# Which engine issues the DMAs that send off ScalarE's results, in a four-layer selective-scan kernel

## The chip, the cores and the metric

The kernel runs on one core of one Trainium2 chip. The metric is the device time of one execution in microseconds (us), the median of several runs. The core's engines have their own instruction streams, in order: TensorE (PE; its weight loads are the row PEld), VectorE (DVE), ScalarE (ACT), GpSimd (POOL) and SyncE (SP), which computes nothing and here issues every DMA.

## What is computed

The input is x, 2 images of 96 channels x 96 x 96. Four layers follow each other; each adds to x what it makes of x's group norm:

```python
x = x + _L0_conv_ref(_gn(x), ...)   # windows of 6 x 6, sampled at learned offsets
x = x + _L1_conv_ref(_gn(x), ...)   # gated sum of four directions
x = x + _L2_conv_ref(_gn(x), ...)   # rows and columns in snake order
x = x + _L3_conv_ref(_gn(x), ...)   # rows and columns, plain order
```

Every layer projects to 192 channels, makes delta, B and C from them, and runs a selective scan in four directions over the 9216 pixels of each image (layer 0: over its windows), with 16 states for each channel:

```python
dA = exp(delta * A); h = h * dA + (delta * u) * B; y = sum over states of h * C
```

The four directions are summed (with D * u), normed or gated, multiplied by silu(z), and projected back to 96 channels. All is float32.

## The kernel before, in words

**Jobs and steps.** A job is one direction over one chunk of T positions (T = 288 in layer 0, class Windows, 256 jobs; T = 384 in layers 1 to 3, Gated, Snake and Plain, 192 jobs each). `Machine.scan` (L385) runs the jobs of a machine, one after the other, in steps; a job has 8 of them (4 groups of 4 states, two halves of 96 channels). Layer 0 has a machine of its own; the other three share a second one and follow each other without a break.

One step n holds, for 128 partitions (32 channels x 4 states, three such blocks side by side): the products dB = w * B on DVE (tile `pd`), the scan on DVE (`hs`), three exponentials on ACT that make `dA` of the next step, and, from the second machine on, two small ACT copies that carry the state from chunk to chunk: `hc`, the scan's last column, and `w`, that column put at the ends of the next w tile. POOL multiplies the scan by C (`hC`), and PE sums over the states (`py`) and spreads B over the partitions (`pb`).

**The preamble** (L321) makes what a job's scan needs, some 10 to 19 steps ahead, a piece a step. PE projects the job's input (`pm`), ACT copies the result to the tile `p` (its rows 64 to 79 are C), and C is stored to a scratch tensor in HBM. PE and ACT then make `v`, delta, with a softplus at its end; it is stored to HBM too. POOL multiplies v by the input, and the product `du` is stored as well. These three are read back by the loads C<-C, d<-delta and w<-du, which spread one row over several partitions: in each job 4 loads of C and, in `spread` (L396), 6 of d and 6 of w, three for each half. In Gated C is multiplied by the gate on POOL before it is stored (L334).

**Sums and directions.** `Cross.jobs_of` (L949) holds what the trunk's jobs do at their end. For direction 0 and 2 ACT copies the sum from PSUM to `y`, and `store` (L990) sends it to HBM (`yc`, `yr`). For direction 1 DVE adds the sum stored before, PE turns the result, ACT copies it to `turn`, and it goes to `yt`. Direction 3 reads those back and ends in the layer's output.

**Stages.** Before a layer's scans can begin, its input is prepared in chunks: normed, projected, filtered, passed through silu. `stage_conv` (L1076) does that for Snake and Plain and stores `flat` and `sz`; every sixth chunk `leave` (L937) stores the columns gathered in the tile `big` to `flatc`, a piece a step. `Gated.stage` (L1191) stores `xn`, the gates `gc` and `gr`, `sz` and, through `leave`, `xc`. The first of these stages runs alone, before the second machine's scans begin (`at_once`, L1397); the rest runs in the background of the scans.

**The order of the work.** The order on each engine is that in which the program is written: the class `Engine` (L146) ties each instruction to the one before it on its engine. Generators are advanced once a step, in `scan`, in a fixed order: first the loads, sums, exponentials and copies of the step, then the ACT work that `act` (L260) put off from the step before (`slot`), then DVE's products and scan, then the preambles, then the background (`hop`, L531). All instructions go through the helper at L156, so the profile shows L156 for nearly every one, and groups are told apart by their tiles.

**What holds SP.** SP takes its DMAs in the program's order. A store waits until its tile is made, and every DMA behind it waits with it. Buffers are few: one `v`, two `p`, three or four `d` and `w`, three C tiles, three slots of each scratch tensor in HBM.

Of the kernel before, what the change touches and what calls it, by code (L numbers as in the profile page):

```python
# [145 lines left out]
class Engine:  # L146


    def __init__(self, tc, engine):
        self.tc, self.engine, self.last = tc, engine, None  # L150
# [61 lines left out]
class Machine:  # L212
# [6 lines left out]

    def __init__(self, ctx, tc, nc, const, T, dram):
        self.tc, self.nc, self.const, self.T, self.dram = tc, nc, const, T, dram
        self.E = E = 0 if T == 288 else 1
        pool = lambda name, bufs, **k: ctx.enter_context(tc.tile_pool(name=f"T{T}{name}", bufs=bufs, **k))
        self.w = pool("w", 1)
        self.sb = pool("sb", 2)
        self.pm = pool("pm", 1, space=PSUM)
        self.pb = pool("pb", 1, space=PSUM)
        self.pd = pool("pd", 1, space=PSUM)  # L230
        self.py = pool("py", 2, space=PSUM)
        if not E:
            self.po = pool("po", 1, space=PSUM)
        self.B = [self.pb.tile([128, 512], F32, tag=f"pb{i}", name="pb") for i in range(2)]
        self.bg, self.low = [], []
        self.turn = 0
        self.now, self.taken, self.used, self.slot = None, None, None, []
# [83 lines left out]
    def preamble(self, j, n):  # L321


        nc, k, layer = self.nc, j.k, j.layer
        T, E = self.T, self.E
        yield from j.gather(j)
        xs = j.xs

        j.p = self.p[n % 2]
        self.own()  # L330
        m = self.mm(self.ps(80)[:, :T], [(layer.wx[:, k, h, :], xs[:, h, :]) for h in range(2)])
        self.act(lambda m=m: nc.scalar.copy(j.p[:, E : E + T], m))
        yield
        if j.gate is not None:  # L334
            C = j.p[64:80, E : E + T]
            nc.gpsimd.tensor_mul(C, C, j.gate[64:80])
            yield
        j.C = self.dram.tile([N, T], F32, tag=f"C{T}", name="C", bufs=3)
        nc.sync.dma_start(j.C, j.p[64:80, E : E + T])
        v = self.t2("v", 1)  # L340
        for h in range(2):
            self.own()
            m = self.mm(self.ps()[:, :T], [(layer.dtw[:, k, 96 * h : 96 * h + 96], j.p[:R, E : E + T])])
            c = layer.scol[:, 2 * k + h : 2 * k + h + 1]
            self.act(lambda h=h, m=m, c=c: nc.scalar.activation(v[:, h, :], m, AF.Identity, bias=c))
            if h == 0:
                yield
        self.act(lambda: nc.scalar.activation(v, v, AF.Softplus))
        yield
        scratch = lambda tag: self.dram.tile([2, 96, T], F32, tag=f"{tag}{T}", name=tag, bufs=3)  # L350
        j.delta, j.du = scratch("delta"), scratch("du")
        nc.sync.dma_start(j.delta.rearrange("h p t -> p h t"), v)
        yield
        du = self.t2("du", 1)
        nc.gpsimd.tensor_mul(du, v, xs)
        nc.sync.dma_start(j.du.rearrange("h p t -> p h t"), du)
        if E:
            j.h = self.sb.tile([128, NG, 3], F32, tag="hc", name="hc", bufs=3)
        yield
        if j.gate is not None:  # L360
            nc.gpsimd.tensor_mul(xs, xs, j.gate.unsqueeze(1).to_broadcast([96, 2, T]))
# [539 lines left out]
class Cross(Layer):  # L901
# [35 lines left out]
    def leave(self, im, c, to, hs):  # L937

        if c % self.group < self.group - 1:
            return  # L940
        rows = slice(4 * (c - self.group + 1), 4 * (c + 1))
        for h in range(hs):
            for w in range(0, S, 16):
                at = slice(w, w + 16)
                self.nc.sync.dma_start(to(h, at, rows), im.big[:, h, at, :])
                yield


    def jobs_of(self, im):  # L949
        nc, T, nch = self.nc, self.T, self.nch  # L950
        jobs = []
        for way in range(4):
            order = range(nch)[:: -1 if way % 2 else 1]
            for c in order:
                at = slice(T * c, T * (c + 1))

                def gather(j, way=way, c=c):
                    assert im.staged, (self.n, im.b, self.now, im.__dict__.get("at"))
                    return self.gather(im, j, way, c)

                def late(j, g, way=way, c=c, at=at):
                    if way == 3 and g == 2:
                        j.turned = self.sb.tile([S, 4, 192], F32, tag="turned", name="turned", bufs=1)
                        nc.sync.dma_start(j.turned, im.yt[4 * c : 4 * c + 4].rearrange("r c k -> c r k"))
                    if way % 2 and g == 5:
                        j.old = self.t2("old", 1)
                        o = (im.yc if way == 1 else im.yr)[:, :, at]
                        nc.sync.dma_start(j.old, o.rearrange("h p t -> p h t"))

                def add(j, h, q, yp, way=way):  # L970
                    if q == 0 and (self.n == 1 or way == 2):
                        nc.tensor.matmul(yp, self.diag[:, h, :], j.xs[:, h, :], start=True, stop=False)
                        return True
                    if q > 1 and way == 3:
                        for r in (2 * q - 4, 2 * q - 3):
                            eye = self.const["rev" if self.snake and r % 2 == 0 else "eye"]
                            nc.tensor.matmul(
                                yp[:, S * r : S * r + S], j.turned[:, r, 96 * h : 96 * h + 96], eye,
                                start=False, stop=False,
                            )  # L980
                    return False

                def finish(j, h, yp, way=way, c=c):
                    if h == 0:
                        j.y = self.t2("y", 3)
                    self.finish(j, way, h, yp, j.y)
                    if h:
                        self.m.bg.append(store(j.y, way, c))

                def store(y, way, c):  # L990
                    at = slice(T * c, T * (c + 1))
                    yield
                    if way == 3:
                        yield from self.end(im, c, y)
                        return
                    if way != 1:
                        nc.sync.dma_start((im.yc if way == 0 else im.yr)[:, :, at].rearrange("h p t -> p h t"), y)
                        return
                    turned = self.sb.tile([S, 4, 192], F32, tag="turn", name="turn", bufs=1)
                    for h in range(2):  # L1000
                        yield from self.spare()
                        p = self.px()
                        for i in range(4):
                            nc.tensor.transpose(
                                p[:, S * i : S * i + S], y[:, h, S * i : S * i + S], self.const["eye"]
                            )
                        nc.scalar.copy(
                            turned[:, :, 96 * h : 96 * h + 96], p[:, : 4 * S].rearrange("p (i k) -> p i k", i=4)
                        )
                        yield  # L1010
                    nc.sync.dma_start(im.yt[:, 4 * c : 4 * c + 4, :], turned)

                jobs.append(
                    Job(self, self.ks[way], way % 2 == 1, c == order[0], gather, finish, late if way % 2 else None, add)
                )
        return jobs
# [59 lines left out]
    def stage_conv(self, im):  # L1076
        nc, T, b = self.nc, self.T, im.b
# [25 lines left out]
        def tail(c, tiles):  # L1103
# [4 lines left out]
            yield  # L1108
            yield
            for t, to in zip(tiles, (im.flat, im.sz)):  # L1110
                nc.sync.dma_start(to[:, :, T * c : T * (c + 1)].rearrange("h p t -> p h t"), t)
            while im.left < c:
                yield
            big = self.columns(im, c)
# [57 lines left out]
class Gated(Cross):  # L1172
# [18 lines left out]
    def stage(self, im):  # L1191
# [12 lines left out]
        def chunk(c):  # L1204
# [17 lines left out]
            self.act(lambda: affine(big, xn.rearrange("p (r c) -> p c r", c=S)))  # L1222
            yield
            yield
            nc.sync.dma_start(im.xn[:, T * c + 3 : T * c + T + 3], o)

            z = self.t2("cz")
            for h in range(2):
# [40 lines left out]
            self.act(lambda: nc.scalar.activation(g.rearrange("p k r -> p r k"), e, AF.Exp))  # L1269
            yield  # L1270
            yield
            nc.sync.dma_start(im.gc[:, :, 4 * c : 4 * c + 4].rearrange("k c r -> c k r"), g)
            p, act = yield from self.either(16)
            nc.tensor.transpose(p[:, :S], g.rearrange("p k r -> p (k r)"), self.const["eye"])
            gt = self.sb.tile([16, S], F32, tag="gt", name="gt")
            act(lambda p=p: nc.scalar.copy(gt, p[:, :S]))
            yield
            yield
            nc.sync.dma_start(im.gr[c], gt)
            yield from self.step(7, 0, 4)  # L1280
            self.act(lambda: nc.scalar.activation(z, z, AF.Silu))
            yield
            yield
            nc.sync.dma_start(im.sz[:, :, at].rearrange("h p t -> p h t"), z)
            yield from self.leave(
                im, c, lambda h, w, r: im.xc[:, 3 : L + 3].rearrange("p (c r) -> p c r", r=S)[:, w, r], 1
            )
# [179 lines left out]
```

## Time and profile before

| what | value |
|---|---|
| median of 3 runs | 29051.85 us (29048.37 to 29093.39) |
| the profiled execution's own time | 29109.88 us |
| its span, and granted TensorE clock | 29108.1 us, 0.646 |
| DVE busy | 25162.6 us (86%) |
| PE busy, PE weight loads | 22199.9 us (76%), 6987.2 us (24%) |
| ACT busy | 18935.5 us (65%), of which 2837 table loads 3639.9 us |
| POOL busy | 18851.4 us (65%) |
| DMA packets' share of the 16 engines' span | 42.7% on one queue, q1 |
| DVE scan, Snake and later | 2.57 us each; product `pd` 1.37 us |

The page gives the busy time of each engine over the whole span, and groups of instructions by tiles as out<-in. Waits are put down to what ended them: "ACT dA <- DMA d<-delta" is idle time of ACT before a dA instruction that the landing of the load of d ended. SPq is SP's queue: an issue that waits. Durations of DMA issues on SP are those of the issue, not of the transfer; the time to landing is given apart.

### The profile page before, as it was taken

The numbers are of one execution on the slowest core, as the hardware profiler recorded it, in microseconds if no ns is written. First come the engines' busy times: TensorE is split into PE (matmuls) and PEld (weight loads), VectorE is DVE, ScalarE is ACT, GpSimd is POOL, SyncE is SP. The second block draws the span as 40 slices with busy tenths as digits, with TensorE's granted clock in tenths as the row PEclk, the third lists the DMA queues.
The fourth block names the chain that finished last, engine by engine and source line by source line (L and its number), as shares of the span: only waits on it lengthen the run. The fifth ranks groups of instructions, "written<-read, shape, count | busy, mean of one in ns | idle before, by whom it ended". The sixth has DMA issues, their size and how long they took to land. (4 is left out here: it accounts for less than half of the span.)

```text
span 29108.1 us, 269563 instructions
## 1 busy us (share of the span) xinstructions
PE 22199.9 (76%) x72312; PEld 6987.2 (24%) x72312; DVE 25162.6 (86%) x15459; ACT 18935.5 (65%) x40441; POOL 18851.4 (65%) x9508
## 2 busy tenths in 40 slices
PE   7887888888567777777777777777777778776778
PEld 2222333333112222222222221212222122221112
DVE  7888888888457788877889999999999989999999
ACT  5666666666567676676666776566765666665566
POOL 5777767777446566765676666666666656666667
PEclk7666666666566676777776675556765577555556
DMA  3333333333344445444444544454444544444444
GB/s 97 101 101 101 101 97 100 98 100 97 69 95 128 125 129 147 149 134 133 136 145 147 147 143 135 142 157 143 145 142 143 155 143 141 146 140 134 134 134 141
DMA packets 3285863, 3707.11 MB, mean 127 GB/s; under 512 B 756928, under 2 KB 3260518, under 8 KB 3284232
## 3 DMA queue, kind: packets, MB, share of 16 engines
q1 hardware_dynamic: 3284328, 3689.86, 42.7%
q8 instruction: 570, 9.34, 0.1%
q14 instruction: 965, 7.91, 0.1%
HBM read 2933.04 MB, written 755.57 MB: 127 GB/s over the span
## 5 line engine op out<-in xcount | busy, mean ns | idle before, releaser
L156 POOL TENSOR_TENSOR hC<-hs,C 128x1152 f32<-128x1152 f32 (+1 forms) x6656 | 15603.3, 2345 | 8616.7 <-PE py L156 4214.1
L156 DVE TENSOR_TENSOR_SCAN hs<-dA,pd 128x1158 f32<-128x1158 f32 (+1 forms) x6656 | 15830.0, 2378 | 1059.8 <-ACT hc L156 115.2
L156 ACT ACTIVATE dA<-d,w_alog 128x384 f32<-128x384 f32 (+1 forms) x19968 | 10306.6, 580 | 6643.8 <-DVE hs L156 5725.8
L156 PE MATMUL py<-hC,zs 128*32 128x384 f32 (+1 forms) x39936 | 7797.5, 677 | 2754.2 <-POOL hC L156 2648.8
L156 DVE TENSOR_TENSOR pd<-w,pb 128x1158 f32<-128x1158 f32 (+1 forms) x6656 | 8465.7, 1272 | 1624.9 <-PE pb L156 548.7
L156 PE MATMUL pb<-p,sel 16*128 16x386 f32 (+1 forms) x6656 | 4151.6, 715 | 485.3 <-ACT cz L156 172.1
L156 ACT ACT_TABLE_LOAD x2837 | 3639.9, 1283 | 108.6 <-DMA w_alog<-in_L_alog 44.4
L156 PE MATMUL pm<-p,w_dtw 6*96 6x384 f32 (+1 forms) x3328 | 2237.7, 768 | 1714.6 <-ACT p L156 982.8
L156 PEld LDWEIGHTS py<-hC,zs 128*32 128x32 f32 x39936 | 1212.2, 129 | 7886.4 <-POOL hC L156 4900.9
L156 PE MATMUL pm<-x,w_in 128*96 128x384 f32 (+1 forms) x2554 | 1514.6, 747 | 996.4 <-ACT p L156 802.9
L156 PEld LDWEIGHTS pb<-p,sel 16*128 16x128 f32 x6656 | 1363.4, 254 | 2681.9 <-issue 1009.7
L156 PE MATMUL pm<-x,w_taps 96*96 96x384 f32 x3456 | 1508.1, 580 | 42.0 <-ACT xs L156 23.8
L156 PE MATMUL po<-xp,w_off 96*96 96x288 f32 x4608 | 1443.3, 460 | 26.8 <-ACT t L156 25.0
L156 PE MATMUL pm<-xs,w_wx 96*80 96x384 f32 x2304 | 1398.6, 753 | 46.3 <-DVE o L156 16.1
L156 PEld LDWEIGHTS pm<-p,w_dtw 6*96 6x96 f32 x3328 | 588.5, 230 | 3328.4 <-ACT p L156 1474.0
L156 ACT COPY w<-hc 128x6 f32<-128x6 f32 x4416 | 830.5, 194 | 499.7 <-DMA w<-du 458.9
L156 ACT ACTIVATE v<-pm,w_scol 96x384 f32<-96x384 f32 (+1 forms) x1664 | 910.3, 547 | 245.9 <-PE pm L156 171.3
L156 POOL TENSOR_TENSOR du<-v,xs 96x768 f32<-96x768 f32 x576 | 1045.0, 1814 | 10.5 <-ACT v L156 10.5
L156 PEld LDWEIGHTS pm<-x,w_in 128*96 128x96 f32 (+1 forms) x2554 | 562.9, 243 | 1973.5 <-ACT p L156 1001.0
L156 PEld LDWEIGHTS po<-xp,w_off 96*96 96x96 f32 x4608 | 791.6, 181 | 658.1 <-issue 342.0
L156 PEld LDWEIGHTS pm<-x,w_taps 96*96 96x96 f32 x3456 | 611.1, 192 | 938.8 <-issue 721.4
L156 ACT COPY hc<-hs 128x3 f32<-128x3 f32 x4608 | 830.7, 180 | 5.7 <-DVE hs L156 5.7
(213 smaller groups left out, 13159.9 us busy)
## 6 DMA issues: line engine op xcount, KB each, us to landing
d<-delta SPq DMA_DIRECT2D x3456, 192.0 KB, 3.3
w<-du SPq DMA_DIRECT2D x3456, 192.0 KB, 3.4
C<-C SPq DMA_DIRECT2D x2304, 192.0 KB, 3.4
d<-delta SPq DMA_DIRECT2D x1536, 144.0 KB, 2.6
w<-du SPq DMA_DIRECT2D x1536, 144.0 KB, 2.6
delta<-v SPq DMA_DIRECT2D x576, 288.0 KB, 2.7
du<-du SPq DMA_DIRECT2D x576, 288.0 KB, 3.4
C<-C SPq DMA_DIRECT2D x1024, 144.0 KB, 2.7
```

Of the source, the lines that this page charges most:

```text
L156: r = traced(*args, **kwargs)
```

## The change

The stores of what ScalarE has made last are issued by ScalarE's own instruction stream instead of SyncE's. These are C where it is not gated, delta, the sums of directions 0 and 2, the turned sums, and the stages' rows, columns, gates and silu(z). Loads stay on SP, and so do the stores of du, of the gated C, of Snake's `ysum` and of the layers' outputs, which other engines make or finish. Nothing else changes; the positions in the program's order are the same.

```diff
@@ preamble
-        nc.sync.dma_start(j.C, j.p[64:80, E : E + T])
+        (nc.scalar if j.gate is None else nc.sync).dma_start(j.C, j.p[64:80, E : E + T])
...
-        nc.sync.dma_start(j.delta.rearrange("h p t -> p h t"), v)
+        nc.scalar.dma_start(j.delta.rearrange("h p t -> p h t"), v)
@@ leave
-                self.nc.sync.dma_start(to(h, at, rows), im.big[:, h, at, :])
+                self.nc.scalar.dma_start(to(h, at, rows), im.big[:, h, at, :])
@@ jobs_of, store
-                        nc.sync.dma_start((im.yc if way == 0 else im.yr)[:, :, at].rearrange("h p t -> p h t"), y)
+                        nc.scalar.dma_start((im.yc if way == 0 else im.yr)[:, :, at].rearrange("h p t -> p h t"), y)
...
-                    nc.sync.dma_start(im.yt[:, 4 * c : 4 * c + 4, :], turned)
+                    nc.scalar.dma_start(im.yt[:, 4 * c : 4 * c + 4, :], turned)
@@ stage_conv, tail
-                nc.sync.dma_start(to[:, :, T * c : T * (c + 1)].rearrange("h p t -> p h t"), t)
+                nc.scalar.dma_start(to[:, :, T * c : T * (c + 1)].rearrange("h p t -> p h t"), t)
@@ Gated.stage
-            nc.sync.dma_start(im.xn[:, T * c + 3 : T * c + T + 3], o)
+            nc.scalar.dma_start(im.xn[:, T * c + 3 : T * c + T + 3], o)
...
-            nc.sync.dma_start(im.gc[:, :, 4 * c : 4 * c + 4].rearrange("k c r -> c k r"), g)
+            nc.scalar.dma_start(im.gc[:, :, 4 * c : 4 * c + 4].rearrange("k c r -> c k r"), g)
...
-            nc.sync.dma_start(im.gr[c], gt)
+            nc.scalar.dma_start(im.gr[c], gt)
...
-            nc.sync.dma_start(im.sz[:, :, at].rearrange("h p t -> p h t"), z)
+            nc.scalar.dma_start(im.sz[:, :, at].rearrange("h p t -> p h t"), z)
```

## The prediction, made before the changed kernel ran

> **What bounds the kernel now.** I read the busy time of each engine stage by stage first, because the page's average (DVE 86%) hides that the stages differ. The boundaries are where the scans of a stage start and end. Columns after the stretch and its length: busy us (instructions) of PE, PEld, DVE, ACT, POOL, then the clock, the DMA share and GB/s.
>
> ```profile
> 0.00:7644.00 7644.00, 6117.86 (x22754) 2269.89 (x22754) 6542.28 (x4915) 4695.90 (x8829) 5362.07 (x3027) 0.65 0.34 99
> 7644.00:8279.00 635.00, 264.89 (x548) 99.93 (x542) 28.22 (x76) 355.90 (x529) 62.10 (x168) 0.50 0.35 38
> 8279.00:15784.00 7505.00, 5728.54 (x18078) 1794.36 (x18079) 6182.19 (x3403) 5163.86 (x10781) 4819.78 (x2431) 0.72 0.46 137
> 15784.00:22436.00 6652.00, 5058.59 (x15670) 1432.18 (x15669) 6190.69 (x3604) 4432.10 (x10601) 4220.60 (x1881) 0.62 0.48 144
> 22436.00:29108.00 6672.00, 5029.98 (x15270) 1390.82 (x15269) 6219.22 (x3464) 4287.75 (x9704) 4386.86 (x2003) 0.60 0.46 141
> ```
>
> The rows are Windows, the staging before Gated's scans ("staging"), Gated, Snake and Plain. VectorE (DVE) sets the pace: 86%, 82%, 93% and 93% in the scan stages. All its idle time is 1102, 600, 1330, 461 and 451 us in that order. ScalarE (ACT) is 61%, 56%, 69%, 67% and 64% busy: second to DVE nowhere but close to the path where its work comes in heaps, in Gated above all.
>
> Next I read who waits for whom: first SP's own waits, then ACT's and DVE's in Gated (us in total, times, longest).
>
> ```profile
> SPq L156 <- ACT w L156: 6342.3, 873, 18.8
> SPq L156 <- ACT v L156: 3095.3, 393, 19.6
> SPq L156 <- DMA du<-du: 2075.6, 832, 4.9
> SPq L156 <- DMA delta<-v: 1454.4, 832, 2.7
> SPq L156 <- ACT p L156: 1270.2, 285, 73.6
> SPq L156 <- ACT y L156: 922.6, 250, 14.0
> ```
>
> SP stands before ACT's results: v, p and y (5288 us) and, in smaller rows of the same view, cz, o, gg and gt (260.6, 213.8, 112.4, 12.9), 5888 us in all. Those waits leave SP with the change. The largest, ACT w, is a load waiting for its buffer and stays.
>
> ```profile
> ACT dA L156 <- DMA d<-delta: 589.7, 192, 9.3
> ...
> ACT w L156 <- DMA w<-du: 256.0, 186, 5.2
> ...
> DVE pd L156 <- ACT w L156: 286.2, 174, 10.5
> ```
>
> These are the two places where a late load shows in Gated: ACT idles 846 us before d and w, and DVE feels some of it through w.
>
> **What leaves SP, and what that gains.** 2528 of SP's 19506 issues move: 832 delta, 640 C (the 192 of Gated stay), 288 y (yc, yr), 144 yt, 96 flat, 144 sz, 192 flatc, 48 each of xc, xn, gc and gr. Summing their own durations in the trace gives 949 us of SP issue. The Trainium skill, DMA: Bandwidth & Descriptors, section "Issuing engines are not separate DMA queues", speaks against more than that: DMAs of all issuers run on the same 16 engines, and a second issuer saves only the sequencer's issue time. The waits row would promise up to 5888 us by standing SP free, the rule only part of 949. So I took every idle time over 0.15 us of ACT, DVE or PE that a landing load ended, and followed SP back from that load while its issues stood end to end. The run's head is almost always a w<-du load that waits for du to land, or a d or w load that waits for its buffer; it is a moved store in single cases only. In the runs stand 185 us of moved issues: 0 in Windows, 15 in staging, 49 in Gated, 67 in Snake, 54 in Plain. That bears out the rule: the loads behind delta wait for delta's landing (1454.4 us over 832) whoever issues it, and delta goes out 0.02 to 0.03 us after the softplus already. What of the 185 reaches DVE: in Gated DVE waits 306 us for w and dA (286.2 and 20.0) against ACT's 846, so 36%; in Snake 38 of 161 us, 23%; in Plain 33 of 299, 11%. 49 x 0.36 + 67 x 0.23 + 54 x 0.11 = 39 us; with staging's 15 whole, a gain of 54 us. Bounds: 0; and 185 whole, plus 43 for DVE's late x strips in Windows (55.8 less its first wait of 12.7), 228 us.
>
> **What each issue costs ACT.** No DMA on ACT is in this trace. The nearest rows are the same step's on SP; here twice the softplus that makes delta.
>
> ```profile
> 10021.22 0.84 ACT L156 ACTIVATE v<-v 96x768 f32<-96x768 f32 x1
> 10021.97 0.18 ACT L156 COPY w<-hc 128x6 f32<-128x6 f32 x1
> 10022.08 0.32 SPq L156 DMA_DIRECT2D delta<-v  x1
> 10022.17 1.28 ACT L156 ACT_TABLE_LOAD   x1
> ...
> 10023.46 1.63 ACT L156 ACTIVATE dA<-d,w_alog 128x384 f32<-128x384 f32 x3
> ...
> 10024.99 0.18 ACT L156 COPY hc<-hs 128x3 f32<-128x3 f32 x1
> 10025.26 2.57 DVE L156 TENSOR_TENSOR_SCAN hs<-dA,pd 128x1158 f32<-128x1158 f32 x1 [0.20 <-ACT hc L156]
> ```
>
> Start us, duration, engine, operation. After the change the delta issue stands between v and the copy into w, and waits for v on ACT itself. Queued behind it are w (DVE's pd waits for it), the table load, the next step's three dA and the hc copy (the scan waits for both). The price of one such "draining" issue: ACT loses the 0.09 us by which v and the copy overlap here, waits 0.02 (v ends at 10022.06, SP starts at 10022.08), issues for 0.31 (median of delta; C 0.318, y 0.311) and starts again 0.04 later (after an ACT semaphore wait that idled it the next instruction starts 0.04 later): 0.46 us. In this step the end of hc sets the scan, so DVE pays all of it. In Snake the same step leaves room: dA ends at 11.21, its scan starts at 13.12.
>
> ```profile
> 20009.58 1.63 ACT L156 ACTIVATE dA<-d,w_alog 128x384 f32<-128x384 f32 x3
> ...
> 20013.12 2.57 DVE L156 TENSOR_TENSOR_SCAN hs<-dA,pd 128x1158 f32<-128x1158 f32 x1
> ```
>
> There 1.91 us of room cover 0.46, and nothing is paid. Over all steps the room between dA's end and its scan is 2.6 to 3.5 us in the median, in Gated under 0.2 us for the tightest tenth.
>
> C, delta and y drain (SP issues them 0.02 us after the producer, in the median). The others (yt, flat, sz, flatc, xc, xn, gc, gr) are written a yield or more after their data: SP issues them 3 to 27 us after (gc 0.9, xn 2.2). For these the skill, Advanced Engine Details and Errata, section "Sequencer Loop", says that engine instructions can be read and queued while microcode executes: the datapath works on, price 0. But the trace shows how short that lead is: an ACT semaphore instruction ends 0.28 us (median) before the next ACT instruction starts, against some 0.40 of issue. I take 0.20, between 0 and a draining issue of 0.55 (0.40 plus the 0.15 above).
>
> How many are paid? ACT gets 2528 issues, 1760 draining, 768 other: 1760 x 0.46 + 768 x 0.20 = 963 us, but most falls into its 5726 us of waiting for the scans. To separate, I followed each of DVE's 1909 idle times over 0.15 us (2747 us together) back through its releasers to the DVE instruction before, and counted the moved issues that lie inside an ACT part of that path, at the time SP issues them now. Draining ones: 36 in Windows (33 delta), 148 in Gated, 33 in Snake, 26 in Plain, 243 in all. Others: 176 in Gated (149 are flat and sz of Snake's staging), 81 in staging, 12 else, 269. So 243 x 0.46 = 112 and 269 x 0.20 = 54: a loss of 166 us. Ends: 243 x 0.31 and nothing for the others, 75; 243 x 0.7 and 269 x 0.55, 318.
>
> One piece is counted by itself: in staging the six xc stores stand together on SP, one burst over 14.87 us (at 7941.34). On ACT they come one a round between compute: 24 at the tile's median 0.59, 14 us; 0 to 59 (four bursts whole).
>
> What remains costs nothing: descriptors, bytes and the loads on SP are the same. du stays on SP behind POOL and the d loads, so POOL's and SP's order to each other changes only by the gaps. If ACT's cover in Snake and Plain were gone, their 1342 issues would cost up to 1342 x 0.46 = 617 us; 1.9 us of room say they don't.
>
> **Sum.** 166 + 14 - 54 = +126 us on the profiled execution's 29109.88 (span 29108.1 and 1.8 around it): 29236. That execution is 58 us above the median of the runs, 29051.85, so I forecast 29052 + 126 = 29178, say 29180.
>
> **Rivals.**
> - *Late loads come forward (faster).* In Gated SP's heaps of d and w issue set the path: 378 loads late there. If the moved issues ahead of them and those behind it pass whole to DVE (228 us), and ACT's price is at its low end, 75, the time is 29052 - 153 = 28900. It decides from the point where the gain of 54 passes the loss, that is if DVE gets over three quarters of it. For it: 5888 us of SP's standing; against: no run's head is a moved store. Chance 0.23, mostly nearer -90 (28960).
> - *All of it falls into ACT's idle time.* Then DVE's waits stay, and the time is within 58 us, 29052. For it: 35% of ACT is idle; against: 324 moved issues on the path in Gated. 0.14.
> - *An issue is dearer on ACT than on SP*, because two issuers meet (SP issues 36% of the span) or it queues full, as flatc (up to 1.69 us) and xc (up to 4.54) do: with 0.3 us more on each of the 512, +154, and the burst whole, +45: about 29380. 0.15.
> - *It doesn't move at all* can't be: every line edited runs.
>
> **Chances.** Some 0.2% (58 us) is what a measurement of this kernel can tell from no change. The likeliest case, +126, has 0.48: its own range is 29070 to 29330, and 0.08 of it falls within 58 us. Slower: 0.40 + 0.15 = 0.55. Same: 0.14 + 0.08 = 0.22. Faster: 0.23. The range takes the loss's high end with the burst (318 + 59 = 377, 29430) and reaches most of the way to the gain's end: 28930.
>
> **What would show it.** Right: ACT's issues appear at 0.31 us with 0.02 before and 0.04 after; SP's rows for v, p and y are gone and C<-C loads go out sooner, with nobody waiting less; the row of d<-delta keeps most of its 590 us in Gated; DVE's waits for ACT (w, hc, dA) grow there, by some 100 us. Snake and Plain change by under 40 us each. Wrong: if d and w waits in Gated fall by half, SP's standing did delay loads, in a way that its runs did not show. If Windows loses more than 50 us, the C and delta issues reach DVE through PE (its pm and pb matmuls wait for ACT's p and v), which I counted only where DVE already waits.

## The result, and the profile after

The changed kernel takes 29023.84 us (median of 16 runs, 29006.44 to 29044.35); the kernel before takes 29112.42 us on the same chip (16 runs, 29048.37 to 29169.14). The ratio is 0.9969, with a 95% interval of 0.9962 to 0.9976: about 90 us, or 0.31%, **faster**. The forecast was 29180 us and slower. The time lies in the predicted range, the direction does not. Run again later, on one chip with new runs of the kernel before, the same kernel gained less: 0.9987 (0.9977 to 0.9997; after2 below). The profiled execution took 29007.22 us (span 29005.0, clock 0.649).

Busy time by stage after the change, in the columns of the prediction's first fence (Windows, staging, Gated, Snake, Plain):

```profile
157.00:7572.00 7415.00, 5924.64 (x22554) 2193.13 (x22552) 6511.07 (x4853) 4661.37 (x8783) 5334.79 (x2987) 0.66 0.34 101
7572.00:8188.00 616.00, 257.70 (x545) 96.77 (x542) 29.37 (x77) 355.46 (x529) 62.24 (x169) 0.51 0.36 40
8188.00:15649.00 7461.00, 5763.07 (x18077) 1809.52 (x18078) 6179.94 (x3403) 5178.17 (x10779) 4819.36 (x2430) 0.72 0.47 137
15650.00:22327.00 6677.00, 5073.84 (x15668) 1437.35 (x15667) 6189.19 (x3603) 4468.06 (x10598) 4219.64 (x1880) 0.62 0.48 143
22328.00:28978.00 6650.00, 5028.66 (x15242) 1388.67 (x15240) 6213.89 (x3456) 4313.83 (x9691) 4377.68 (x1996) 0.60 0.47 141
```

From the first scan of a stage to its last, before and after: Windows 7488.1 to 7414.7 (-73), staging 637.0 to 615.9 (-21), Gated 7501.4 to 7460.6 (-41), Snake 6650.0 to 6676.5 (+26), Plain 6645.0 to 6649.5 (+5). DVE's work is the same in each; what changed is how long it stands. In these two executions the largest piece is in Windows, for which the forecast had only a loss.

The moved issues appear on a queue of their own (page, part 3: packets, MB, share of 16 engines). The two shares add up to 43.1%, against 42.7% on q1 alone before: the traffic is the same.

```profile
q1 hardware_dynamic: 2566248, 3207.82, 36.4%
...
q10 hardware_dynamic: 718080, 482.05, 6.7%
```

SP's own waits (us in total, times, longest):

```profile
SPq L156 <- DMA delta<-v: 8075.2, 832, 82.8
SPq L156 <- POOL hC L156: 5646.1, 1380, 9.7
SPq L156 <- DMA du<-du: 2220.1, 832, 7.0
```

The rows for v, p and y are gone or next to nothing (p 0.8 us), as forecast. But SP does not stand less: all its rows add up to 19048 us, against 17854 before. It now stands before delta's landing (8075.2 us over the same 832 loads, 1454.4 before), most likely because the d load behind delta's store comes up for issue earlier and waits for the same data. The row "ACT w", 6342.3 us before, which I said would stay, shrinks to 10.1 us, while "POOL hC" grows from 400.0 to 5646.1: a row names only the last of several releases.

In Gated, ACT's waits (first fence) and DVE's (second):

```profile
ACT dA L156 <- DMA d<-delta: 518.9, 192, 8.6
...
ACT w L156 <- DMA w<-du: 205.1, 180, 5.7
...
ACT w L156 <- ACT v L156: 55.3, 135, 0.9
...
ACT L156 <- DMA w<-du: 20.0, 6, 4.3
...
ACT w L156 <- DMA d<-delta: 14.7, 5, 5.2
```

```profile
DVE pd L156 <- ACT w L156: 238.0, 177, 7.2
DVE pd L156 <- PE pb L156: 186.2, 142, 3.5
DVE hs L156 <- ACT hc L156: 110.5, 117, 1.7
DVE pd L156 <- ACT hc L156: 83.8, 42, 3.9
```

Loads of d and w do come earlier. The two rows of the prediction's second fence fall from 845.7 to 724.0 us together; part of that only stands in other rows, which are new (the last two of the fence, and 4.4 us at cz). ACT's waits for these loads in all fall from 846 to 763 us, and DVE's wait for w from 286.2 to 238.0. "ACT w <- ACT v" is new too: the price of delta's issue. DVE's waits for hc grow (94.5 to 110.5 and 36.1 to 83.8).

A softplus of delta in Gated, as in the prediction's third fence:

```profile
9966.92 0.84 ACT L156 ACTIVATE v<-v 96x768 f32<-96x768 f32 x1
9967.80 0.31 ACTq L156 DMA_DIRECT2D delta<-v  x1
9968.15 0.20 ACT L156 COPY w<-hc 128x6 f32<-128x6 f32 x1 [0.38 <-ACT v L156]
9968.37 1.28 ACT L156 ACT_TABLE_LOAD   x1
```

The issue starts 0.04 us after v, takes 0.31, and ACT's datapath idles 0.38 us where the two instructions overlapped by 0.09 before.

### The profile page after: what moved, and what is told of

Read it like the earlier page. It is cut to its first block, busy times and chain, and to the rows that moved or that the text cites. A ratio compares the mean times of both kernels' runs of the same rounds, so it can differ in the third digit from the quotient of the medians.

```text
span 29005.0 us, 268196 instructions
## 1 busy us (share of the span) xinstructions
PE 22131.0 (76%) x72312; PEld 6968.5 (24%) x72312; DVE 25159.9 (87%) x15459; ACT 19020.5 (66%) x40441; POOL 18853.2 (65%) x9508
```

## The experiments

Two theories of the gain. **Late loads**: SP, rid of 2528 issues, gets the loads out earlier (the prediction's first rival). **Clock**: in Windows TensorE's granted clock swings, and the change shifts ScalarE against that swing. Each kernel below is the kernel before with the edit named; times are medians, ratios against runs of the kernel before on the same chip. Lengths of stages are of single profiled executions.

### Windows: what the profile shows

Windows does its work in strips of 64 scans. Most of them take close to 232.1 us in both kernels. Before, 11 of 31 took over 236 us; after, 1. Here are the first 25 us of three neighbouring strips before (busy PE, PEld, DVE, ACT, POOL, then the clock, DMA share and GB/s), which go on to take 239.0, 245.3 and 232.8 us:

```profile
3635.50:3660.50 25.00, 25.00 (x72) 11.25 (x70) 14.57 (x12) 9.82 (x18) 9.50 (x6) 0.58 0.20 58
3874.50:3899.50 25.00, 25.00 (x63) 10.98 (x64) 12.91 (x10) 9.81 (x18) 8.29 (x5) 0.50 0.20 58
4119.80:4144.80 25.00, 24.94 (x112) 12.06 (x110) 21.19 (x17) 13.58 (x26) 14.36 (x8) 0.91 0.32 95
```

And the two strips of the changed kernel that lie at the same place, 232.2 and 232.1 us long:

```profile
3643.50:3668.50 25.00, 24.94 (x116) 12.36 (x116) 21.86 (x17) 13.91 (x26) 14.30 (x8) 0.97 0.33 96
3875.60:3900.60 25.00, 24.94 (x116) 12.41 (x115) 22.22 (x17) 13.91 (x26) 14.39 (x8) 0.97 0.28 82
```

A strip begins with a heap of PE work (the offset matmuls `po` of the next strip), on which DVE waits. Where the clock is 0.5 to 0.6 there, PE gets through 63 to 72 matmuls instead of 112 to 116, and DVE does 13 to 15 us of work instead of 21 to 22. The same matmuls, before (first) and after; the bracket is DVE's wait before the instruction:

```profile
3880.25 4.16 PE L156 MATMUL po<-xp,w_off 96*96 96x288 f32 x8
...
3886.83 0.67 DVE L156 TENSOR_TENSOR yn<-y,py 96x288 f32<-96x288 f32 x1 [3.93 <-PE py L156]
```

```profile
3879.67 2.18 PE L156 MATMUL po<-xp,w_off 96*96 96x288 f32 x8
...
3883.20 0.69 DVE L156 TENSOR_TENSOR yn<-y,py 96x288 f32<-96x288 f32 x1 [0.33 <-PE py L156]
```

Eight matmuls of one shape take 4.16 us or 2.18. The record of the clock alternates between 0.5 and 1.0 in multiples of 3.413 us, and its pattern repeats with the strip (correlation with itself 232 us later: 0.75 before, 0.86 after; 232.1 us are 68 of these 3.413). The strips differ in when the clock rises: before, within 4.3 us of the strip's start in the short ones, and 17.4 to 34.5 us after it in all 11 long ones. PE is recorded as busy throughout those 17 to 35 us, so its busy time doesn't tell what delays the rise; that stays open. That a late rise makes a strip long holds in all 20 profiles that have Windows: of 600 strips (the first of each profile left out) 52 had a clock under 0.66 in their first 25 us, and all took over 236 us; the other 548 had 0.90 or more, and 6 of them took over 236.

### Windows: which part of the change does it

**w_only**: only Windows' C and delta move. **l0_before, l0_after**: Windows alone (the other three layers are left out), in the two orders, each run in two sets.

```diff
-        nc.sync.dma_start(j.C, j.p[64:80, E : E + T])
+        (nc.sync if E else nc.scalar).dma_start(j.C, j.p[64:80, E : E + T])      # E is 0 in Windows alone; delta alike
```

w_only, as expected: 

> Only Windows' C and delta (512 of the 2528 issues) move to ScalarE; the other three layers issue everything on SP as before. Theory 1 (loads come forward in Gated because SP no longer stands before ScalarE's results): Windows has no late loads, so the time stays within 30 us of the kernel before, or 10 to 30 us above it for ScalarE's price. Theory 2 (in Windows the gain is one of the TensorE clock: strips whose first 25 us are granted about 0.55 instead of 0.95 take 239 to 245 us instead of 232, and the new order makes them rarer): 40 to 80 us faster, and the profile shows Windows' scans in some 7415 us instead of 7488.

l0_before: 

> Layers 1 to 3 are left out: the kernel ends with layer 0's output; the order of before. It times Windows alone. Expected 7.66 to 7.70 ms; by theory 2 the runs scatter by tens of us as strips fall into a low clock or not, by theory 1 they agree as well as other kernels do.

l0_after: 

> Layers 1 to 3 are left out again, with the order of the change. By theory 1 within 15 us of the same layer with the order of before, or slower by up to 30. By theory 2 some 40 to 75 us faster in the median, with strips of 232 us nearly throughout and less scatter.

l0_before2: 

> Layers Gated, Snake and Plain are left out, so that only Windows runs, in the order of the kernel before. A second set of runs: 7600 to 7690 us, with a wide scatter (30 us or more between lowest and highest), if the row of strips that begin at a low clock comes and goes between executions.

l0_after2: 

> The same with C and delta issued by ScalarE. Theory of the clock: median 20 to 60 us below that of Windows alone in the order of before, and a narrower scatter. If Windows has no part in the gain, the two medians are within 10 us.

w_only: 29089.1 us, ratio 0.9970 (0.9959 to 0.9981), and no strip over 236 us, about as the theory of the clock expected. Windows alone in the order of before: eight runs from 7596 to 7692 us, mean 7645; with C and delta on ScalarE: eight runs from 7585 to 7627 us, mean 7606. The difference is -39 us (95%: -69 to -10), -38 in the first set and -41 in the second; in the first, 40 to 75 was expected. (A ninth run of the first kind, 7735 us, is not counted; with it the difference would be -49.) The mean clock separates the two kinds wholly: 0.651 to 0.661 against 0.662 to 0.665. So Windows gains by itself, and it is the scatter upwards that goes.

**w_dummy**: no DMA moves; where the change would issue C and delta, ScalarE copies 96 elements into an unused tile, which shifts it by a few tenths of a us. **l0_dummy**: the same with Windows alone. **w_dum1**: only the copy at C.

```diff
         nc.sync.dma_start(j.C, j.p[64:80, E : E + T])
+        if not E:
+            dum = self.sb.tile([96, 96], F32, tag="dum", name="dum", bufs=1)
+            nc.scalar.copy(dum[:R], j.p[:R, E : E + 96])
...
         nc.sync.dma_start(j.delta.rearrange("h p t -> p h t"), v)
+        if not E:
+            nc.scalar.copy(dum, v[:, 1, :96])
```

w_dummy: 

> All DMAs stay on SyncE as in the kernel before; in Windows alone ScalarE makes a copy of 96 elements into an unused tile at the two places where the change would make it issue C and delta. Theory of the clock (Windows' gain is that its strips no longer begin in a stretch of low granted TensorE clock, which any small shift of ScalarE can bring about): 40 to 90 us faster than before, with at most 4 of the 31 strips longer than 236 us. Theory of the freed queue (Windows gains because SyncE no longer stands behind C and delta, so that the loads behind them go out earlier): no gain, 0 to 30 us slower, and 9 or more strips longer than 236 us. From Gated on nothing should change by more than 20 us.

w_dum1: 

> All DMAs as in the kernel before; in Windows ScalarE makes one copy of 96 elements where the change would make it issue C, and none for delta: half the shift of the kernel with two copies. If any shift of ScalarE breaks the row of strips that begin at a low granted clock, at most 3 strips are longer than 236 us and the kernel is 30 to 90 us faster than before; if it takes a shift of about the size of both issues, 4 or more strips are long and it is within 30 us of before. From Gated on no change over 20 us.

l0_dummy: 

> Windows alone (the other three layers left out), all DMAs on SyncE as before, but ScalarE makes a copy of 96 elements at each of the two places where the change would make it issue C and delta. If the shift of ScalarE does it: median 20 to 60 us below Windows alone in the order of before. If SyncE's being free does it: within 10 us of it, or above.

w_dummy: 29092.41 us, ratio 0.9982 (0.9973 to 0.9991), no strip over 236 us. l0_dummy: five runs from 7597 to 7622 us, mean 7608, at clocks of 0.663 to 0.667, where l0_after has 7606. With every DMA still on SP, a shift of ScalarE alone gives as much as the change does in Windows alone; in the whole kernel it gives 0.18% against w_only's 0.30%, with intervals that overlap. So the freed SP isn't needed for this gain, though a smaller part of it isn't ruled out. w_dum1 gives nothing: ratio 1.0001 (0.9992 to 1.0010). Its profiled execution has one long strip, but it was the fastest of ten runs (29071.89, median 29124.35). A single profile can't size Windows: in eight profiles of kernels with Windows in the order of before, it took from 7397 to 7499 us, with 1 to 12 long strips (mean 5.3); in nine with C and delta on ScalarE 7396 to 7430, with 0 to 3 (mean 1.4).

### The trunk: staging and Gated

**trunk_only**: the whole change except Windows' C and delta. **g_delta**: only Gated's delta moves. **g_stores**: only the stages' stores that feed Gated and Snake, and Gated's y and yt. **g_both**: the last two together.

```diff
-        nc.sync.dma_start(j.delta.rearrange("h p t -> p h t"), v)
+        (nc.scalar if j.layer.n == 1 else nc.sync).dma_start(j.delta.rearrange("h p t -> p h t"), v)   # g_delta, g_both
...
-                nc.sync.dma_start(to[:, :, T * c : T * (c + 1)].rearrange("h p t -> p h t"), t)
+                (nc.scalar if self.n == 2 else nc.sync).dma_start(to[...], t)    # g_stores, g_both; y, yt, xn, gc, gr, sz alike
```

trunk_only: 

> Windows issues all on SP as before; all else moves as in the change. Theory 1: nearly the whole gain, 60 to 100 us faster, with the first stage 20 us and Gated 40 us shorter and Snake some 25 us longer. Theory 2: 20 to 45 us faster (the first stage -21, Gated -41, Snake +26, Plain +5 of the profiles add to -31), and Windows keeps strips of 239 to 245 us.

g_delta: 

> Only Gated's delta goes out from ScalarE, all else as before. Theory of the loads that come forward: the waits dA<-DMA d and w<-DMA w in Gated fall by 60 us or more together and Gated is 20 to 50 us shorter. Theory of the prediction on record (a draining issue costs ScalarE 0.46 us and nothing comes forward that counts): Gated 20 to 40 us longer. Windows keeps its long strips (9 or more over 236 us), Snake and Plain stay within 10 us.

g_stores: 

> Only the stores of the stages and Gated's sums (y and its turned form) go out from ScalarE; every C and delta stays on SyncE. If the staging between Windows and Gated and the loads of Gated gain from SyncE's being free of these, staging is 15 to 20 us shorter and Gated 10 to 30 us shorter; by the prediction on record it is within 15 us of no change in both. Together with the kernel that moves Gated's delta alone it should add up to the 40 to 65 us by which Gated was shorter in the whole change; if the two add up to much less, one needs the other.

g_both: 

> Gated's delta and all the stores that feed or leave Gated go out from ScalarE together; C and delta of the other layers, and the sums of Snake and Plain, stay on SyncE. The two moves apart gave Gated about -15 us and about +10 us, the whole change -40 to -65. If one needs the other (the loads of d and w come forward only when SyncE is rid of both), Gated is 40 us or more shorter than in the kernels that leave it alone (7535 to 7547) and the wait dA<-DMA d falls below 540 us. If they merely add up, Gated is within 15 us of 7535, and its gain in the whole change has come from something that reaches it from Windows or is chance. Staging 15 to 25 us shorter in both cases. Windows as before, with any number of long strips.

trunk_only came out at 0.9989 (0.9983 to 0.9996), some 31 us faster, with 12 long strips: what the theory of the clock expected of a kernel without Windows' part.

| kernels | ratio (95%) | ACT's waits for loads of d and w in Gated, us | DVE's waits for w, hc, dA in Gated, us | Gated, us | staging, us |
|---|---|---|---|---|---|
| Gated as before (5 profiles) | | 863 (840 to 887) | 462 | 7532 (7501 to 7547) | 651 (637 to 657) |
| g_delta | 0.9993 (0.9983 to 1.0002) | 836 | 452 | 7518 | 658 |
| g_stores | 0.9992 (0.9983 to 1.0001) | 848 | 426 | 7544 | 628 |
| g_both | 0.9985 (0.9976 to 0.9994) | 810 | 412 | 7505 | 639 |
| trunk_only | 0.9989 (0.9983 to 0.9996) | 794 | 442 | 7478 | 640 |
| Gated as changed (8 profiles, these two among them) | | 791 (764 to 810) | 409 | 7499 (7461 to 7522) | 636 (616 to 641) |

The third column counts all idle time of ACT that a load of d or w ended, in whatever row it stands. Single lengths of Gated scatter by 45 us and more, so those of g_delta, g_stores and g_both decide nothing: they fall between the ranges that the three expectations named. The means do decide: Gated is 33 us shorter with the change (95%: 8 to 58). Staging is some 15 us shorter.

DVE's idle time tells more when it is sorted by the eight steps of a job, because the moves act in different steps and each step scatters little (us in Gated, ranges over the profiles):

| step of the job | as before (5) | g_delta | g_stores | g_both | as changed (8) |
|---|---|---|---|---|---|
| 0 | 100 (89 to 106) | 100 | 132 | 121 | 123 (116 to 129) |
| 1 | 245 (237 to 254) | 223 | 212 | 192 | 185 (170 to 199) |
| 5 | 129 (128 to 129) | 146 | 130 | 148 | 149 (147 to 151) |
| the other five | 879 | 871 | 890 | 865 | 862 |

Step 1 is where DVE waits longest for ACT's w, and so for loads: 212 us of it before, 193 with delta moved, 175 with the stores moved, 158 with both. Each move brings the loads forward, and the two add up (22 and 33 us alone, 53 together): neither needs the other. Against this stand two prices. Step 5 loses 20 us to delta's issue (DVE's wait for hc there goes from 48 to 67 us, and g_stores doesn't have it). Step 0 loses 23 us to the stores (g_delta doesn't have it).

### Snake and Plain

**sp_cd**: only C and delta of these two layers. **keep_y**: the whole change, but their y and yt stay on SP. **keep_cd**: the whole change, but their C and delta stay. **no_flat**: the whole change, but the pairs flat and sz of Plain's staging stay on SP (14 lie in Snake's third quarter, 10 in its fourth, 14 in Plain's first); those of Snake's own staging, 22 of which lie in Snake's first quarter, go out from ScalarE. **after2** is the changed kernel and **keep_cd2** is keep_cd, on one chip.

```diff
-        (nc.scalar if j.gate is None else nc.sync).dma_start(j.C, ...)
+        (nc.scalar if j.layer.n < 1 else nc.sync).dma_start(j.C, ...)      # keep_cd; delta: n < 2
...
-                nc.scalar.dma_start(to[:, :, T * c : T * (c + 1)].rearrange("h p t -> p h t"), t)
+                (nc.scalar if self.n == 2 else nc.sync).dma_start(to[...], t)      # no_flat
```

sp_cd: 

> Only C and delta of Snake and Plain go out from ScalarE. If these are what made Snake longer in the whole change, Snake is 20 to 30 us longer than before, Plain 0 to 15 us longer, and DVE's waits for hc from ScalarE grow by 30 us or more in Snake; if it was the sums y instead, Snake stays within 10 us. Windows and Gated stay as before.

keep_y: 

> The whole change, but the sums of Snake and Plain (y and its turned form) stay on SyncE. If these 384 stores are what made Snake 26 us longer, Snake is back within 8 us of 6650, Plain within 8 us of 6646, and the kernel is 20 to 30 us faster than the changed kernel (ratio to before about 0.996). If it was C and delta, Snake stays at 6670 or more. Windows has at most 3 strips over 236 us, Gated 7460 to 7485.

keep_cd: 

> The whole change, but C and delta of Snake and Plain stay on SyncE. If the sums made Snake longer, Snake stays at 6670 or more; if C and delta, it is back within 8 us of 6650; if it takes both together, it is back within 8 us in this kernel and in the one that keeps the sums. Windows has at most 3 strips over 236 us, Gated 7460 to 7485.

no_flat: 

> The whole change, but the stage's rows flat and sz that go out while Snake runs (the store in the loop over tiles ahead of the columns) stay on SyncE; C, delta, the sums and the columns flatc still go out from ScalarE. In the changed kernel these two stores fall in behind C's issue, so that ScalarE issues three DMAs in a row (1.25 to 1.37 us) ahead of the copy w<-hc for the next step. If that row of three is what made Snake 26 us longer, Snake comes back to 6630 to 6650 and Plain to 6633 to 6650, and the kernel is 25 to 60 us faster than the whole change (ratio to before 0.995 to 0.996). If it is C and delta in Snake as such, together with any other issue, Snake stays at 6665 or more.

after2: 

> The changed kernel itself, run again on the chip of the next one, so that the two can be set side by side: ratio to before 0.996 to 0.998. Snake's first quarter (384 scans) 1683 to 1690 us, as in every kernel that issues both C and the rows flat and sz from ScalarE there.

keep_cd2: 

> The whole change with C and delta of Snake and Plain left on SyncE, again. If the row of three issues costs what Snake and Plain show (6631 and 6633 us where the changed kernel has 6677 and 6650), this kernel is 35 to 65 us faster than the changed kernel on the same chip, ratio to before 0.995 to 0.9965; Snake's first quarter 1664 to 1669 us. If that difference is chance, the two agree within 15 us.

| kernel | ratio (95%) | Snake, us | of it quarters 1 and 3 | Plain, us | of it quarter 1 |
|---|---|---|---|---|---|
| before | | 6650 | 1669, 1691 | 6645 | 1702 |
| sp_cd | 0.9994 (0.9985 to 1.0004) | 6635 | 1666, 1681 | 6647 | 1701 |
| keep_y | 0.9985 (0.9976 to 0.9995) | 6677 | 1685, 1699 | 6660 | 1711 |
| keep_cd | 0.9964 (0.9952 to 0.9975) | 6631 | 1668, 1673 | 6633 | 1694 |
| no_flat | 0.9965 (0.9951 to 0.9979) | 6673 | 1686, 1689 | 6632 | 1693 |
| after2 | 0.9987 (0.9977 to 0.9997) | 6677 | 1688, 1695 | 6656 | 1705 |
| keep_cd2 | 0.9959 (0.9945 to 0.9974) | 6642 | 1661, 1687 | 6640 | 1697 |

The sums y are innocent (keep_y). C and delta alone cost Snake nothing (sp_cd: 15 us less, where its expectation had 20 to 30 more or at most 10 either way), nor do the rows without them (keep_cd); together they cost 26 us in Snake. The changed kernel's timeline of ACT says why:

```profile
15862.83 0.48 ACT L156 COPY p<-pm 80x384 f32<-80x384 f32 x1
15863.34 0.32 ACTq L156 DMA_DIRECT2D C<-p  x1
15863.69 0.44 ACTq L156 DMA_DIRECT2D flat<-cz  x1
15864.16 0.47 ACTq L156 DMA_DIRECT2D sz<-cz  x1
15864.67 0.20 ACT L156 COPY w<-hc 128x6 f32<-128x6 f32 x1 [1.37 <-DVE pd L156]
```

The same two stores in keep_cd:

```profile
15885.26 0.62 ACT L156 ACTIVATE dA<-d,w_alog 128x384 f32<-128x384 f32 x1
15885.28 0.31 ACTq L156 DMA_DIRECT2D flat<-cz  x1
15885.63 0.47 ACTq L156 DMA_DIRECT2D sz<-cz  x1
15885.78 1.11 ACT L156 ACTIVATE dA<-d,w_alog 128x384 f32<-128x384 f32 x2
```

In keep_cd both issues run while the first exponential computes, and the datapath loses nothing: this holds for 48 of 48. In the changed kernel they stand behind C's issue, which has drained the datapath, so nothing is running that could cover them: ACT idles 1.37 us for the three, in the median of 48. Against C's own 0.39 the pair costs 0.98 us. 22 such pairs lie in Snake's first quarter, 22 x 0.98 = 22 us; that quarter takes 1686 us in the mean of the five kernels of this kind and 1667 in that of the ten others. DVE's idle time puts it down to the jobs with a pair: in Snake's first half they have 4.25 to 4.45 us each in these five kernels and 3.12 to 3.57 in the ten others, while jobs without a pair have 1.9 to 2.0 everywhere. In its second half the difference is smaller (4.29 to 4.42 in the four kernels that have such pairs there, 3.17 to 4.13 in the others), so the 48 pairs together stay below 48 x 0.98 = 47 us; why it is smaller there I can't show. no_flat takes away the later pairs: beside the others of its kind Plain's first quarter is 12 to 18 us shorter (14 pairs, 14 us), Snake's third 6 to 10 shorter; Snake's first, where the pairs remain, stays at 1686. My expectation for it, Snake at 6630 to 6650, missed: the edit reached only half of Snake's pairs, the half that costs less. DVE's wait for hc in Snake, changed kernel and then keep_cd:

```profile
DVE hs L156 <- ACT hc L156: 44.2, 59, 1.7
```

```profile
DVE hs L156 <- ACT hc L156: 9.5, 14, 1.0
```

keep_cd is faster than the kernel before (0.9964 and 0.9959) and than the changed kernel: on one chip 29010.98 us against 29101.97 (means 72 us apart, 95%: 33 to 110; 35 to 65 was expected). after2, at 0.9987, gained less than the 0.996 to 0.998 that I expected of it.

## Why the prediction was wrong

| stage | forecast, us | measured, means of profiles, us |
|---|---|---|
| Windows (36 x 0.46) | +17 | -22 |
| staging (16 + 14 - 15) | +15 | -15 |
| Gated (103 - 18) | +85 | -33 |
| Snake (33 x 0.46 - 67 x 0.23) | 0 | +26 |
| Plain (26 x 0.46 - 54 x 0.11) | +6 | +6 |

**Gated, the largest miss: the loss of 103 us (148 x 0.46 + 176 x 0.20) was counted too high, the gain of 18 (49 x 0.36) too low.** By the steps of the job, the loss was 43 us (20 from delta's issue, 23 from the stores) and the gain 60 in step 1, with 17 more in the other steps.

*The loss.* The price of a draining issue on ACT, 0.46 us, was right: delta's idles ACT 0.38 us and loses the overlap of 0.09, 0.47 together, in the median of Gated's 192. But DVE lost 20 us to these 192, 0.10 each. Which of ACT's other waits covered the rest is not shown. y was counted as draining and isn't: on ACT yc and yr are issued 0.45 us before the compute ahead of them ends, because another activation stands between y's copy and its store and is still running; the next instruction starts with its usual overlap of 0.10. The same holds for flat and sz in Gated, where C is not on ACT, and for yt in Gated and Snake, in the median. The 149 issues of flat and sz that the forecast counted there can't be a count of issues: only 24 of flat and 24 of sz from Snake's staging go out while Gated runs, 72 with Gated's own sz, so some were counted behind more than one of DVE's waits. And on ACT they cost nothing: the price of 0 that I drew from the Trainium skill, Advanced Engine Details and Errata, section "Sequencer Loop" (other engine instructions can be read and queued while microcode executes), was right for them, and I put 0.20 against it.

*The gain.* I counted only runs of issues that stood end to end up to the load, 49 us. The 60 us of step 1 are more than those 49 whole, so issues further ahead, with a gap between, held back the loads too. The Trainium skill's rule (DMA: Bandwidth & Descriptors, "Issuing engines are not separate DMA queues") that a second issuer saves only issue time isn't contradicted: 552 issues moved in Gated, and all 2528 hold 949 us on SP, 0.38 each, so 207 us of issue left SP there, more than was gained. It was I who cut it down too far. The first rival had this mechanism, at a chance of 0.23.

**Windows was given only a loss.** It gained. The step that failed is the reading of the stage's mean clock (0.65) as if PE's pace were constant: in a third of the strips the clock rose 17 to 35 us into PE's heap and not at its start, which the strips' lengths would have shown. The text named a loss of over 50 us through PE as a sign of error; what came was a gain through PE. Its size is not settled: 22 us in the mean of the profiles, 39 in Windows alone, 76 (57 to 95) in w_only's runs, mean against mean. Why ScalarE's shift breaks the pattern, and one of half the size does not, I can't show.

**Snake: pieces were priced one by one.** The pair flat and sz is free behind an exponential and costs ACT 0.98 us behind C; the forecast had no such term.

**Staging:** which of its three terms was wrong, these runs don't separate.

The forecast was +126 (the last 2 are issues outside these stages); the stages' means give -22 - 15 - 33 + 26 + 6 = -38, the first set of runs -90 (ratio 0.9969), the last -38 (0.9987). That the last agrees with the means is in part luck. What separates the two sets is probably Windows, which varies from execution to execution; that isn't shown. That the time still fell within the range is luck as well: the range was wide, and the terms of Gated and Windows had the wrong sign or size.

## What to carry to other kernels

Before pricing a stage by its averages, list the lengths of its repeated units and the granted clock at the start of each: if equal units differ with the clock, some of the time hangs on when the clock rises, which a small shift of one engine may change, and only repeated runs, or a dummy shift, tell it from the change's own effect. Price a DMA issue on a compute engine by what stands ahead of it in program order: behind data made long ago and a long instruction in flight it is free, behind an instruction that waits for the engine's own last result it costs its full time, and so do all issues that follow in the same row. When loads are late, count all issue time that leaves their queue, not only what touches them, and count each issue once. To tell a price from a gain that meet in one stage, sort the bounding engine's idle time by its place in the loop.

## What the runs showed of the hardware

In Windows the granted TensorE clock alternates between 0.5 and 1.0 in multiples of 3.413 us, in a pattern that repeats with the strips of 232 us; strips that begin with a clock under 0.66 take 237 to 251 us. Two ScalarE copies of 96 elements in each of Windows' jobs, which compute nothing that is used, made the whole kernel 0.18% faster (0.09 to 0.27); one copy changed nothing (1.0001). In Snake and Plain an issue of C on ScalarE idles its datapath for 0.39 us, with two further DMAs behind it for 1.37 us; the same two behind a running exponential idle it for nothing (48 of 48).
